# Cross-attention block on one core: the loads and the order of the first 30 microseconds rearranged

## The chip, the cores and the metric

The kernel runs on one core of one Trainium2 chip. The time is device microseconds of one execution; before the change it was 1048.52 us, the median of 3 runs (1047.92 to 1049.07). The engines are named as the profile names them: PE (TensorE, matrix products; PEld is its weight load), DVE (VectorE), ACT (ScalarE), POOL (GpSimd) and SP (SyncE, which issues nearly all DMAs; SPq is that issuing). Each engine runs its own instructions in the order in which the kernel wrote them, and waits at the head of its queue for what the instruction needs.

## The reference: what is computed

All data are float32: x is (16, 1024, 512), the context (16, 64, 512), the condition (16, 512). There are 16 heads of 32.

```python
def _ada_ln(x, c, W_ss, b_ss):
    h = (x - mean(x)) / sqrt(var(x) + 1e-5)
    ss = silu(c) @ W_ss + b_ss
    scale, bias = split(ss, 2)
    return (1 + scale)[:, None, :] * h + bias[:, None, :]

xq  = _ada_ln(x,   t_vec, Wss_q,  bss_q)
xkv = _ada_ln(ctx, t_vec, Wss_kv, bss_kv)
q = xq @ Wq + bq
k, v = split(xkv @ Wkv + bkv)
attn = softmax(q k^T / sqrt(32))          # for each batch and head
out = x + (attn @ v) @ Wp + bp
```

## The kernel before

The 16 x 1024 rows of x are cut into 32 blocks of 512 rows, two to a batch. Block i is held as a tile of 128 partitions by 4 row tiles by 512 features (`x_tiles[i]`). The order of all work is written out by hand: each call adds instructions to the queues of the engines it uses, and they stay in that order. The first blocks have an order of their own (a straight list of calls), then a loop runs over blocks 4 to 29, and a list closes the end. The change lies in the loads at the top and in the straight list, up to the query work of block 0.

What is done there, call by call:

- `load_x(i)`, `load_context(b)`, `load_scale_shift` and the loads beside them issue DMAs on SP. The order before is: condition, x_0 (1 MB in one DMA), four short rows of biases (`brow`), the scale's and then the shift's half of the query side's scale-shift weights (`wss_q`, 1 MB each), `w_q_sb` (1 MB), the first context (256 KB), x_1, both halves of the context side's weights (`wss_kv`), `w_kv_sb` (2 MB).
- `pc` (line 208) transposes the condition on PE; ACT and DVE make silu of it.
- `biases()` transposes `brow` on PE into `pb`; DVE copies it to `bias_t`.
- `q_stats(i)` takes mean and variance of the rows on DVE, two instructions for each row tile. `q_scale(i)` makes 1/sqrt of them: two small instructions on ACT and then four on DVE (lines 279 to 294). `hidden(i, ts)` normalises row tiles on ACT (line 324). `kv_stats`, `kv_scale` and `context_hidden` do the same for the context.
- `scale_shift_rows(name, h)` computes the scale (h = 0) or the shift (h = 1) for all 16 batches as 16 products on PE (`pss`), which the profile lists as 32 instructions, and a copy on DVE; `scale_shift(name, off, h)` transposes that copy on PE (`pst`) and adds the bias on DVE.
- `first_features(ts)` transposes normalised row tiles of block 0 on PE (`pxt`, four transposes for each row tile) and copies them out, even row tiles on ACT and odd ones on DVE.
- `query_weights(0)` multiplies w_q's rows by batch 0's scale: two instructions on ACT and two on DVE.
- `queries(i, o)` makes one 128-feature slice of the queries: 4 products on PE that read all four row tiles (8 instructions in the profile, `pq`). `queried(i, o)` copies the slice to `qt` on ACT and adds the bias; with `later=True` `queries` leaves that call to the list.
- The bias of batch-scaled queries is `bqs`: `query_bias_rows` multiplies the shift by w_q on PE (`pbq`) and copies it on DVE; `query_bias` transposes the copy on PE (`pbt`) and adds b_q on DVE.
- `turn(i)` and `move(i)` transpose the row tiles of later blocks with DVE and DMAs.

PSUM decides some of the order. The pool `ps_m` has four single banks, which `bank(name)` hands out in turn; a bank is written again only when what was read from it has been read:

```python
ring = [0, 1, 2, 3]
def bank(name, k=None):
    if k is None:
        k = ring.pop(0)
        ring.append(k)
    return ps_m.tile([P, TB], F32, tag=f"mm{k}", name=name)
```

The pool `ps_s` has two double banks, used later for the scores; `spare(name)` takes the first half of one.

Of the kernel before, what the change touches and what calls it, by code (L numbers as in the profile page):

```python
# [9 lines left out]
F32 = mybir.dt.float32  # L10
# [5 lines left out]
P = 128  # L16
# [4 lines left out]
def cross_attention_block(  # L21
# [51 lines left out]
    nc = tc.nc  # L73

    B, LQ, H = x.shape
# [3 lines left out]
    NC = H // P  # L79
    HPC = P // DH  # L80
    TB = 512
    NT = TB // P
# [8 lines left out]
    xpool = ctx.enter_context(tc.tile_pool(name="xpool", bufs=2))  # L91
    hpool = ctx.enter_context(tc.tile_pool(name="hpool", bufs=1))
    qpool = ctx.enter_context(tc.tile_pool(name="qpool", bufs=2))
    big = ctx.enter_context(tc.tile_pool(name="big", bufs=1))
# [16 lines left out]
# [5 lines that stand above are left out]
# [15 lines left out]
    def load_context(b):  # L131
        t = kvpool.tile([P, H], F32, tag="ctx", name=f"ctx_{b}")
        nc.sync.dma_start(t, context[b : b + 2].rearrange("b k h -> (b k) h"))
        ctx_tiles[b] = t

    def rows_of(a, i):
        b, s = divmod(i, BPB)
        return a[b, s * TB : (s + 1) * TB, :].rearrange("(t p) h -> p t h", p=P)

    def load_x(i):  # L140

        t = xpool.tile([P, NT, H], F32, tag="r" if i == 3 else "x", name=f"x_{i}")
        nc.sync.dma_start(t, rows_of(x, i))
        x_tiles[i] = t

    def load_residual(i):

# [4 lines left out]

    w_ss = {}

    def load_scale_shift(name, w):
        for j in range(2):
            t = big.tile([P, NC, H], F32, tag=f"big{len(w_ss)}", name=f"wss_{name}_{j}")
            nc.sync.dma_start(t, w[:, j * H : (j + 1) * H].rearrange("(c p) o -> p c o", p=P))
            w_ss[name, j] = t

    load_x(0)

# [3 lines left out]
    for src, n in ((b_ss_q, 2 * NC), (b_ss_kv, 2 * NC), (b_q, NC), (b_kv[0:H], NC)):  # L166
        nc.sync.dma_start(brow[at : at + n, :], src.rearrange("(r f) -> r f", f=P))
        at += n
    load_scale_shift("q", w_ss_q)
    w_q_sb = const.tile([P, NC, H], F32, name="w_q_sb")  # L170
    nc.sync.dma_start(w_q_sb, w_q.rearrange("(c p) o -> p c o", p=P))
    load_context(0)
    load_x(1)
    load_scale_shift("kv", w_ss_kv)
    w_kv_sb = const.tile([P, NC, 2 * H], F32, name="w_kv_sb")
    nc.sync.dma_start(w_kv_sb, w_kv.rearrange("(c p) o -> p c o", p=P))

    b_v_sb = const.tile([P, P], F32, name="b_v_sb")

# [27 lines left out]
    for c in range(NC):  # L207
        nc.tensor.transpose(
            pc[:, c * B : (c + 1) * B], c_sb[:, c * P : (c + 1) * P], ident[:B, :B]
        )  # L210
    pcv = pc[:, : NC * B].rearrange("p (c b) -> p c b", c=NC)
    den = early_tile(P, NC * B).rearrange("p (c b) -> p c b", c=NC)
    nc.scalar.activation(den, pcv, AF.Exp, scale=-1.0)
# [8 lines left out]
    def biases():  # L222
        pb = bank("pb")
        nc.tensor.transpose(pb[:, :NBR], brow, ident[:NBR, :NBR])
        nc.vector.tensor_copy(bias_t, pb[:, :NBR])
# [3 lines left out]
    def scale_shift_rows(name, h):  # L229

        pss = bank(f"pss_{name}_{h}")
        for c in range(NC):
            for p in range(NC):
                nc.tensor.matmul(
                    pss[32 * p : 32 * p + 32, :P],
                    lhsT=silu_t[:, c, :],
                    rhs=w_ss[name, h][:, c, p * P : (p + 1) * P],
                    start=(c == 0),
                    stop=(c == NC - 1),
                )  # L240
        ssr[name, h] = early_tile(P, P)
        nc.vector.tensor_copy(ssr[name, h], pss[:, :P])

    def scale_shift(name, off, h):
        pst = bank(f"pst_{name}_{h}")
        nc.tensor.transpose(pst[:, :P], ssr.pop((name, h)), ident)
        if h == 0:
            ss[name] = const.tile([P, 2 * NC, BW], F32, name=f"ss_{name}")
        at = h * NC
        t = ss[name][:, at : at + NC, :]  # L250
        nc.vector.tensor_tensor(
            t,
            pst[:, :P].rearrange("f (p b) -> f p b", p=NC),
            bias_t[:, off + at : off + at + NC].unsqueeze(2).to_broadcast([P, NC, BW]),
            ALU.add,
        )
        if h == 0:
            nc.vector.tensor_scalar_add(t, t, 1.0)
# [40 lines left out]
    def q_stats(i, ts=range(NT), kvb=None):  # L299

        if ts[0] == 0:
            q_mv[i] = small.tile([P, NT + 1, 2], F32, tag="mvq", name=f"mvq_{i}")
        for t in ts:
            row_stats(q_mv[i][:, t, :], x_tiles[i][:, t, :])
        if kvb is not None:
            row_stats(q_mv[i][:, NT, :], ctx_tiles[kvb])

    def q_scale(i, kvb=None):
        n = NT if kvb is None else NT + 1
        q_rstd[i] = rstd_of(q_mv.pop(i)[:, :n, :], n, "q", i > 2)  # L310
        if kvb is not None:
            kv_rstd[kvb] = (q_rstd[i], NT)
# [15 lines left out]
    def hidden(i, ts):  # L328

        for t in ts:  # L330
            normalise(x_tiles[i][:, t, :], x_tiles[i][:, t, :], q_rstd[i], t)
# [8 lines left out]
    def context_hidden(b):  # L340
        hk = kvpool.tile([P, H], F32, tag="hk", name=f"hk_{b}")
        normalise(hk, ctx_tiles.pop(b), *kv_rstd.pop(b))
        hk_tiles[b] = hk

    def spare(name):
        return ps_s.tile([P, 2, TB], F32, tag="s", name=name)[:, 0, :]
# [111 lines left out]
    bqs_rows = early_tile(P, P)  # L458

    def query_bias_rows():  # L460
        pbq = bank("pbq")
        for c in range(NC):
            for o in range(NC):
                nc.tensor.matmul(
                    pbq[32 * o : 32 * o + 32, :P],
                    lhsT=ss["q"][:, NC + c, :],
                    rhs=w_q_sb[:, c, o * P : (o + 1) * P],
                    start=(c == 0),
                    stop=(c == NC - 1),
                )  # L470
        nc.vector.tensor_copy(bqs_rows, pbq[:, :P])

    def query_bias():
        pbt = bank("pbt")
        nc.tensor.transpose(pbt[:, :P], bqs_rows, ident)
        nc.vector.tensor_tensor(
            bqs,
            pbt[:, :P].rearrange("p (o b) -> p o b", o=NC),
            bq_t.unsqueeze(2).to_broadcast([P, NC, BW]),
            ALU.add,  # L480
        )

    def query_weights(b):
        t = qpool.tile([P, NC, H], F32, tag="wq", name=f"wq_{b}")
        if b:
            scale = ss["q"][:, :NC, b : b + 1].to_broadcast([P, NC, H])
            nc.gpsimd.tensor_tensor(t, w_q_sb, scale, ALU.mult)
        else:
            for c in range(NC):
                scale = ss["q"][:, c, b : b + 1]  # L490
                if c % 2:
                    nc.vector.tensor_scalar_mul(t[:, c, :], w_q_sb[:, c, :], scale)
                else:
                    nc.scalar.mul(t[:, c, :], w_q_sb[:, c, :], scale)
        wq_tiles[b] = t
# [26 lines left out]
    def first_features(ts):  # L522
        if 0 in ts:
            xt_tiles[0] = qpool.tile([P, 4, NC, P], F32, tag="xt", name="xt_0")
        for t in ts:
            pt = bank(f"pxt_{t}")
            for c in range(NC):
                nc.tensor.transpose(
                    pt[:, c * P : (c + 1) * P], x_tiles[0][:, t, c * P : (c + 1) * P], ident
                )  # L530
            dst = xt_tiles[0][:, t].rearrange("p c n -> p (c n)")
            if t % 2:
                nc.vector.tensor_copy(dst, pt)
            else:
                nc.scalar.copy(dst, pt)
        if ts[-1] == NT - 1:
            x_tiles.pop(0)
# [3 lines left out]
    def queries(i, o, later=False):  # L541
        xt, b = xt_tiles[i], i // BPB
        w = wq_tiles.get(b, w_q_sb)
        pq = bank(f"pq_{i}_{o}")
        for c in range(NC):
            nc.tensor.matmul(  # L546
                pq.rearrange("p (g n) -> p g n", g=4),
                lhsT=w[:, c, o * P : (o + 1) * P],
                rhs=xt[:, :, c, :],
                start=(c == 0),  # L550
                stop=(c == NC - 1),
            )
        pq_tiles[i, o] = pq
        if not later:
            queried(i, o)
# [414 lines left out]


    q_stats(0)
    q_scale(0)
    hidden(0, range(NT))
    biases()
    scale_shift_rows("q", 0)
    first_features((0, 1))
    scale_shift("q", 0, 0)
    scale_shift_rows("q", 1)
    first_features((2,))  # L980
    scale_shift("q", 0, 1)
    first_features((3,))
    query_weights(0)
    query_bias_rows()
    load_x(2)
    load_value_bias()
    kv_stats(0)
    kv_scale(0)
    queries(0, 0, later=True)
    context_hidden(0)  # L990
    query_bias()
    queried(0, 0)
    q_stats(1)
    q_scale(1)
    hidden(1, (0, 1))
    queries(0, 1)
    hidden(1, (2, 3))
    for h in range(2):
        scale_shift_rows("kv", h)
    turn(1, range(NT))  # L1000
# [388 lines left out]
```

## Time and profile before

| | |
|---|---|
| median of 3 runs | 1048.52 us |
| profiled execution, its own time | 1047.6 us |
| its span, first to last instruction | 1045.5 us |
| PE busy | 1024.9 us, 98% of the span |
| DVE busy | 863.4 us, 83% |
| ACT busy | 611.0 us, 58% |
| POOL busy | 762.1 us, 73% |
| DMA | 147.50 MB, mean 141 GB/s over the span |
| first long run of PE begins | 10.41 us after the span's start |

All durations come from the profiled execution. Matrix products are pipelined and their ends are modelled, so PE's share is an upper view of its work. A line of a timeline reads: start in us, duration in us, engine, line of the kernel, operation, what is written, what is read, shapes, count; in brackets the idle time before it and what ended that. Where a wait is for several things, the profile names the one that came last by its own records, which can be one that the instruction doesn't depend on.

### The profile page before, as it was taken

To read this page: it belongs to the slowest core of one execution; us is meant where nothing else is said; L and a number is where in the kernel's file an instruction comes from. 1 tells how busy PE (TensorE), PEld (TensorE's weight loads), DVE (VectorE), ACT (ScalarE), POOL (GpSimd) and SP (SyncE) were. 2 spreads that over 40 slices of the span, in tenths; PEclk is the share of its full clock that TensorE was granted. 3 is DMA by queue.
4 is the path that set the end of the run, shared out by engine and by line. 5 is a ranking of instruction groups with operands and counts; after the bars stand their busy time and mean duration, and the time that the engine had idled before them with its cause. 6 is when DMAs were issued, how large, how long until landed. Compare 5 with 4: busy or idle time off the path is not lost.

```text
span 1045.5 us, 22774 instructions
## 1 busy us (share of the span) xinstructions
PE 1024.9 (98%) x8986; PEld 744.5 (71%) x8986; DVE 863.4 (83%) x1150; ACT 611.0 (58%) x940; POOL 762.1 (73%) x495
## 2 busy tenths in 40 slices
PE   6999899999999999999999999999999999999998
PEld 4535577778777778778777787777877777877433
DVE  5798978987798887897889877988778897777993
ACT  3656756665566745665746655666556664565330
POOL 0579786886978866988668897688796886798340
PEclk9999999999999999999999999999999999999999
DMA  9850555343455433545435445354445433335202
GB/s 342 248 185 31 165 165 175 121 146 125 142 172 164 126 99 128 164 155 162 123 87 164 155 142 164 100 158 125 139 148 172 144 121 107 102 112 161 82 31 91
DMA packets 101562, 147.50 MB, mean 141 GB/s; under 512 B 32040, under 2 KB 32192, under 8 KB 101456
## 3 DMA queue, kind: packets, MB, share of 16 engines
q1 hardware_dynamic: 100432, 143.95, 43.1%
q0 software_dynamic: 1024, 2.10, 0.9%
q8 instruction: 71, 1.16, 0.5%
q14 instruction: 35, 0.29, 0.1%
HBM read 78.95 MB, written 34.54 MB: 109 GB/s over the span
## 4 chain that ended last, share of the span: by engine, by line
PE 88%; DVE 4%; POOL 4%; issue 2%; ACT 1%; SPq 1%; DMA 1%; DVEq 0%; POOLq 0%
PE pp L949 32%; PE pq L633 30%; PE po L841 6%; PE ps L681 6%; PE pq L546 5%; PE pp L868 3%; PE pv L434 2%; PE pk L398 2%; POOL s L737 1%; DVE m L693 1%; SPq L516 1%; POOL sum L780 1%; DVE s L737 1%; DVE mb L724 1%; DMA x<-in_x_dram 0%
## 5 line engine op out<-in xcount | busy, mean ns | idle before, releaser
L737 POOL TENSOR_TENSOR s<-s,mb 128x2048 f32<-128x2048 f32 x58 | 263.1, 4563 | 160.1 <-DVE mb L724 156.1
L702 ACT COPY s<-ps 128x1024 f32<-128x1024 f32 x128 | 129.5, 1013 | 111.0 <-DVE m L693 71.7
L693 DVE TRANSPOSE_TENSOR_REDUCE m<-ps 128x32 f32<-128x1024 f32 x128 | 150.8, 1215 | 29.6 <-PE ps L681 29.0
L949 PE MATMUL pp<-w_p_sb,ot 128*128 128x256 f32 x696 | 159.8, 379 | 0.0
L663 ACT ACTIVATE qt<-pq,bias_t 128x256 f32<-128x256 f32 x216 | 89.2, 463 | 111.2 <-PE pq L633 108.7
L963 DVE TENSOR_TENSOR r<-pp,r 128x512 f32<-128x512 f32 x203 | 131.6, 670 | 25.0 <-PE pp L949 17.0
L743 ACT ACTIVATE s<-s 128x2048 f32<-128x2048 f32 x64 | 122.3, 1911 | 43.9 <-POOL s L737 32.5
L949 PEld LDWEIGHTS pp<-w_p_sb,ot 128*128 128x128 f32 x696 | 132.1, 190 | 19.0 <-issue 1.0
L780 POOL TENSOR_TENSOR sum<-s,s 128x2048 f32<-128x2048 f32 x29 | 131.7, 4540 | 3.5 <-ACT s L743 3.4
L949 PEld LDWEIGHTS pp<-WT,s 128*128 128x128 f32 x464 | 83.7, 189 | 54.9 <-issue 32.3
L949 PE MATMUL pp<-WT,s 128*128 128x256 f32 x464 | 115.2, 391 | 0.0
L949 PE MATMUL pp<-WT,ot 128*128 128x256 f32 x464 | 109.8, 379 | 2.4 <-ACT pp L912 2.4
L633 PE MATMUL pq<-xt_sums,wq_sums 128*128 128x256 f32 x432 | 104.9, 386 | 0.0
L633 PE MATMUL pq<-xt,wq_sums 128*128 128x256 f32 x432 | 102.8, 381 | 0.8 <-DVE qt L670 0.8
L633 PEld LDWEIGHTS pq<-xt_sums,wq_sums 128*128 128x128 f32 x432 | 79.8, 190 | 32.4 <-issue 22.6
L633 PE MATMUL pq<-xt,w_q_sb 128*128 128x256 f32 x432 | 102.3, 379 | 0.4 <-ACT pq L645 0.4
L949 PEld LDWEIGHTS pp<-WT,ot 128*128 128x128 f32 x464 | 88.0, 190 | 16.0 <-POOL s L928 3.3
L324 ACT ACTIVATE x<-x,rstdq 128x512 f32<-128x512 f32 x128 | 96.5, 807 | 1.9 <-DVE rstdq L294 1.9
L263 DVE BATCH_NORM_STATS2 bs<-x 128x6 f32<-128x512 f32 x128 | 86.9, 679 | 8.0 <-DMA x<-in_x_dram 8.0
L670 DVE TENSOR_TENSOR qt<-pq,qt 128x256 f32<-128x256 f32 x108 | 40.5, 417 | 63.3 <-PE pq L633 62.8
L633 PEld LDWEIGHTS pq<-xt,w_q_sb 128*128 128x128 f32 x432 | 81.9, 190 | 12.7 <-issue 0.8
L633 PEld LDWEIGHTS pq<-xt,wq_sums 128*128 128x128 f32 x432 | 80.5, 190 | 12.4 <-issue 1.2
(135 smaller groups left out, 1661.0 us busy)
## 6 DMA issues: line engine op xcount, KB each, us to landing
x<-in_x_dram SPq DMA_DIRECT2D x32, 1024.0 KB, 5.7
r<-in_x_dram SPq DMA_DIRECT2D x32, 1024.0 KB, 5.4
xt<-ht SPq DMA_DIRECT2D x464, 64.0 KB, 2.0
out_dram<-r SPq DMA_DIRECT2D x58, 512.0 KB, 3.7
out_dram<-r SPq DMA_DIRECT2D x12, 256.0 KB, 2.0
wss_q<-in_L_xcond_Wss_q_dram SPq DMA_DIRECT2D x2, 1024.0 KB, 8.3
ctx<-in_ctx_dram SPq DMA_DIRECT2D x8, 256.0 KB, 3.1
wss_kv<-in_L_xcond_Wss_kv_dram SPq DMA_DIRECT2D x2, 1024.0 KB
```

The costliest lines, as they stand in the source:

```text
L263: nc.vector.bn_stats(bs, r)
L324: nc.scalar.activation(dst, src, AF.Identity, bias=rstd[:, 1, j : j + 1], scale=rstd[:, 0, j : j + 1])
L633: nc.tensor.matmul(qa[k][:, m * HT : (m + 1) * HT].rearrange("p (g n) -> p g n", g=2), lhsT=a[:, c, m * P : (m + 1) * P], rhs=x[:, :, c, : ...
L663: nc.scalar.activation(dst, src, AF.Identity, bias=bq_t[:, o : o + 1])
L681: nc.tensor.matmul(pss[r // 2][32 * c : 32 * c + 32, r % 2, :], lhsT=kt[rows, c, z * HK : (z + 1) * HK], rhs=qt[rows, c, :], start=True, s ...
L693: nc.vector.tensor_reduce(m_tiles[i][:, z, 2 * e : 2 * e + 2, :], pss[e].rearrange("p r (j a) -> p r j a", a=32), AX.X, ALU.max, apply_tra ...
L702: nc.scalar.copy(s_sb[:, 2 * e : 2 * e + 2, :], pss[e])
L737: eng.tensor_tensor(s_tiles[i, z], s_tiles[i, z], mb_tiles[i], ALU.subtract)
L743: nc.scalar.activation(p, p, AF.Exp, scale=SCALE)
L780: nc.gpsimd.tensor_tensor(t, s_tiles[i, 0], s_tiles[i, 1], ALU.add)
L949: nc.tensor.matmul(acc[k][:, t * HO : (t + 1) * HO], lhsT=rows[:, c, t * P : (t + 1) * P], rhs=cols[:, c, :], start=n == 2 and t == 0 and ...
L963: nc.vector.tensor_add(r, acc[k].rearrange("p (t h) -> p t h", t=2), r)
```

## The change

x_0 is loaded in four DMAs of one row tile each. The scale's weights come first, then w_q, then the shift's weights; w_kv comes in two halves by columns. After the condition's transposes PE runs 20 transposes of the identity into an unused double bank of `ps_s` (`warm(20)`), and 8 more after `biases()`, which moves ahead of `q_scale(0)`. The normalising of block 0 is split in two; the features of all four row tiles and the first slice of the queries come ahead of the shift's products; the second slice comes ahead of `query_bias_rows`; `q_stats(1)` and `q_scale(1)` stand between `query_bias_rows` and `query_bias`; the two `queried` follow, and then the normalising of block 1. `pbq` and `pbt` lie in `spare` instead of a bank of the ring.

```diff
     def load_x(i):
-        t = xpool.tile([P, NT, H], F32, tag="r" if i == 3 else "x", name=f"x_{i}")
-        nc.sync.dma_start(t, rows_of(x, i))
-        x_tiles[i] = t
+        x_tile = xpool.tile([P, NT, H], F32, tag="r" if i == 3 else "x", name=f"x_{i}")
+        for ts in [slice(t, t + 1) for t in range(NT)] if i == 0 else [slice(0, NT)]:
+            nc.sync.dma_start(x_tile[:, ts, :], rows_of(x, i)[:, ts, :])
+        x_tiles[i] = x_tile
...
-    load_scale_shift("q", w_ss_q)
+    load_scale_shift("q", w_ss_q, 0)
     w_q_sb = const.tile([P, NC, H], F32, name="w_q_sb")
     nc.sync.dma_start(w_q_sb, w_q.rearrange("(c p) o -> p c o", p=P))
+    load_scale_shift("q", w_ss_q, 1)
     load_context(0)
     load_x(1)
-    load_scale_shift("kv", w_ss_kv)
+    for j in range(2):
+        load_scale_shift("kv", w_ss_kv, j)
     w_kv_sb = const.tile([P, NC, 2 * H], F32, name="w_kv_sb")
-    nc.sync.dma_start(w_kv_sb, w_kv.rearrange("(c p) o -> p c o", p=P))
+    for j in range(2):
+        half = slice(j * H, (j + 1) * H)
+        nc.sync.dma_start(w_kv_sb[:, :, half], w_kv[:, half].rearrange("(c p) o -> p c o", p=P))
...
+    def warm(n):
+        for _ in range(n):
+            nc.tensor.transpose(idle[:, :P], ident, ident)
+    idle = ps_s.tile([P, 2, TB], F32, tag="s", name="idle")[:, 0, :]
+    warm(20)
...
-        pbq = bank("pbq")
+        pbq = spare("pbq")
...
-        pbt = bank("pbt")
+        pbt = spare("pbt")
...
     q_stats(0)
+    biases()
+    warm(8)
     q_scale(0)
-    hidden(0, range(NT))
-    biases()
+    hidden(0, (0, 1))
     scale_shift_rows("q", 0)
-    first_features((0, 1))
+    first_features((0,))
     scale_shift("q", 0, 0)
+    hidden(0, (2, 3))
+    first_features((1,))
+    query_weights(0)
+    first_features((2, 3))
+    queries(0, 0, later=True)
     scale_shift_rows("q", 1)
-    first_features((2,))
     scale_shift("q", 0, 1)
-    first_features((3,))
-    query_weights(0)
-    query_bias_rows()
     load_x(2)
     load_value_bias()
     kv_stats(0)
     kv_scale(0)
-    queries(0, 0, later=True)
     context_hidden(0)
+    queries(0, 1, later=True)
+    query_bias_rows()
+    q_stats(1)
+    q_scale(1)
     query_bias()
     queried(0, 0)
-    q_stats(1)
-    q_scale(1)
-    hidden(1, (0, 1))
-    queries(0, 1)
-    hidden(1, (2, 3))
+    queried(0, 1)
+    hidden(1, range(NT))
     for h in range(2):
         scale_shift_rows("kv", h)
     turn(1, range(NT))
```

## The prediction

> **What bounds the kernel now.** I read four views of the profile in this order: the page, the waits of TensorE (PE), the chain that ended last in order of time, and the timelines of DVE, ACT and SP over the first 45 us, because every edit lies there.
>
> The page first. The span, PE's row, and the chain's shares by engine:
>
> ```profile
> span 1045.5 us, 22774 instructions
> PE 1024.9 (98%) x8986; PEld 744.5 (71%) x8986; DVE 863.4 (83%) x1150; ACT 611.0 (58%) x940; POOL 762.1 (73%) x495
> PE 88%; DVE 4%; POOL 4%; issue 2%; ACT 1%; SPq 1%; DMA 1%; DVEq 0%; POOLq 0%
> ```
>
> PE is busy for 98% of the span, and the chain is PE for 88%. What PE waited for, longest first (total us, times, longest):
>
> ```profile
> PE pb L224 <- DMA early<-in_L_xcond_bkv_dram: 3.8, 1, 3.8
> PE pss_q L234 <- DVE workq L291: 3.1, 1, 3.1
> PE pc L208 <- DMA early<-in_cond_dram: 2.6, 1, 2.6
> PE pp L949 <- ACT pp L912: 2.4, 1, 2.4
> ```
>
> The first three, 9.5 us, are all before 10.41 us. The other waits in that list add up to some 7 us in more than 1000. So from 10.41 us on PE hardly pauses, and a delay of PE in the first 45 us has nowhere to be absorbed: the work of all later blocks moves with it. I therefore measure the change by one number, the start of the first scale-shift product of the context (pss_kv), since from there on both orders give PE the same work. Before, it starts at 24.86, as the chain in order of time shows (start, us, what):
>
> ```profile
> 10.41 1.94 PE pss_q L234 x32
> 12.35 1.90 PE pxt L528 x8
> ...
> 14.46 1.01 PE pss_q L234 x32
> 15.47 0.59 PE pxt L528 x4
> ...
> 17.68 3.63 PE pq L546 x8
> 21.31 0.11 PE pbt L475
> ...
> 24.86 1.89 PE pss_kv L234 x64
> ```
>
> The reader should see two things. PE runs without a hole from 10.41 to 24.86, so reordering alone can win nothing there. And the first 32 pss_q products took 1.94 us, the next 32 of the same form 1.01; eight transposes took 1.90 first, four 0.59 later. PE starts at about half rate for 4 us: 0.93 + 0.72 = 1.65 us is all that starting warm can save.
>
> What ends the wait at 10.41? The list names a DVE instruction on which pss_q doesn't depend. The tile's DMA answers it (two issues; landing min, median, max):
>
> ```profile
> 3.14 0.95 SPq L158 DMA_DIRECT2D wss_q<-in_L_xcond_Wss_q_dram  x2
> DMA to landing us min/median/max: 7.1/8.3/9.4
> ```
>
> 3.14 + 7.1 = 10.24: the scale's weights land just before PE starts. The shift's land at about 13.0, and w_q at 4.13 + 11.6 = 15.7. The DMA engines' share is 0.9 to 1.1 from 3 us to 30 us.
>
> **The change part by part, up to the first queries.** I call A the start of queries(0, 0). *Rows in four parts:* ctx, a 256 KB load of the same shape, took 0.35 us to issue, so four parts cost 4 x 0.39 = 1.6 us on SP instead of 0.45; the four bias rows and the scale's weights behind them are issued 1.1 us later (4.25 instead of 3.14). SP shows one more thing: the tenth DMA (ctx) waited 1.6 us for the second (x_0) to land. With four parts the tenth is the scale's weights, and it would wait for part 0; with x_0's 1 MB landing 5.0 us after its issue, a quarter is there by about 4.2, so this costs nothing or little. Bounds for the landing of wss_q 0: 4.25 + 5.0 (as x_0 had it, alone) = 9.3, and 4.25 + 7.1 = 11.4. The bytes ahead of it are the same and the engines are full from 3 us, so I take 10.4.
>
> [...]
>
> *Statistics of x_0:* a pair of DVE instructions takes 0.79 us; with parts the last pair alone follows the landing at 6.2, so they end at 7.1 instead of 9.51. The bias transpose (biases) now stands ahead of rstd on DVE: it waits on PE for the 20 idle products (4.75 us at the slow 0.24 each, from 3.2) and ends at about 8.5; rstd is ready at 9.3 instead of 10.96. Two hidden tiles at 0.73 are done at 10.8. All of this hides behind the wait for wss_q 0; if that cover went, it would be 10.8 - 10.4 = 0.4 us late. The second set of 8 idle products (2 us at most) ends before 10.4: cost nothing.
>
> *From there to A* ACT decides, not PE, since it runs its instructions in order:
>
> ```profile
> 11.00 2.93 ACT L324 ACTIVATE x<-x,rstdq 128x512 f32<-128x512 f32 x4 [0.82 <-DVE rstdq L294]
> 16.58 1.34 ACT L494 ACTIVATE wq<-w_q_sb,ss_q 128x512 f32<-128x512 f32 x2
> 21.79 0.69 ACT L568 ACTIVATE qt<-pq,bqs 128x512 f32<-128x512 f32 x1 [0.32 <-DVE bqs L476]
> ```
>
> pss_q warm 10.4 to 11.43; transposes of tile 0 to 12.0; their copy on ACT (0.56) to 12.6; hidden of tiles 2 and 3, queued behind that copy, to 14.1; two weight scalings (w_q lands by 13 to 13.6, in the shift's old place) to 15.4; copy of tile 2 to 16.0. queries(0, 0) reads all four tiles, so A = 16.0 instead of 17.68: 1.7 us won. PE now has holes in this stretch (about 13 to 16) where it had none.
>
> **From A to pss_kv, where it is lost.** Before, this took 24.86 - 17.68 = 7.18 us: two queries and a 0.1 transpose. After, PE has more in between: queries 3.63, the shift's pss_q 1.03, a bare wait for its copy on DVE (0.06 + 0.29), the transpose 0.2, queries 3.63, query_bias_rows (pbq) 1.03, and the copy of that on DVE 0.35. That is A + 10.25 = 26.25. And then comes a new wait. bank() hands out four PSUM banks in turn: counted through the new order, pq_0_0 is the ninth and has bank 0, pq_0_1 bank 3, and pss_kv_0, the thirteenth, bank 0 again. It can't be written until queried(0, 0) has read bank 0 on ACT. queried(0, 0) waits for bqs, and bqs stands on DVE *behind* q_stats(1) and q_scale(1), which themselves stand behind the copy of pbq. Their length is in DVE's timeline:
>
> ```profile
> 21.46 0.29 DVE L476 TENSOR_TENSOR bqs<-pbt,bias_t 128x128 f32<-128x128 f32 x1 [0.84 <-PE pbt L475]
> 21.67 0.68 DVE L263 BATCH_NORM_STATS2 bs<-x 128x6 f32<-128x512 f32 x1
> ...
> 25.64 0.17 DVE L291 SCALAR_TENSOR_TENSOR workq<-workq 128x4 f32<-128x4 f32 x1 [0.69 <-ACT workq L280]
> ...
> 26.24 0.17 DVE L294 SCALAR_TENSOR_TENSOR rstdq<-rstdq,mvq 128x4 f32<-128x4 f32 x1
> ```
>
> Before, bqs came first and the 21.67 to 26.41 = 4.74 us of statistics after it cost PE nothing. After: 26.25 + 4.74 + bqs 0.25 + queried 0.70 + 0.06 of hand-overs = 32.0, against 24.86: +7.15 us. PE idles some 5.5 us (only pbt falls in it). Queued behind pss_kv on PE is everything else: queries(0, 2), the keys, the first scores. x_1 lands before 21.67 in the profile, so the statistics wait for no load.
>
> *After such an idle stretch* PE may be slow again as at 10.41 (there after waits of 3.8 and 3.1 us). Bounds: 0, and the 64 pss_kv products at the slow rate, 2 x 1.94 - 1.89 = 2.0. The row of 10.41 is the nearest, so I take 1.8. Moving hidden(1) after both queried costs nothing: four tiles (2.9 us on ACT) run beside the pss_kv products and queries(0, 2). The later order, w_kv in two halves, pbq and pbt in the score banks: nothing that waits; w_kv is used 10 us after pss_kv.
>
> **The sum.** +7.15 + 1.8 = +8.95. The profiled execution took 1047.6 (span 1045.5 and 2.1 around it), so 1056.55; the median of the runs, 1048.52, is 0.92 above that: 1057.5.
>
> [...] In the trace the rate doubled 4 us after 10.41, and half of those 4 us were transposes, so they do not hinder it; whether they alone release it no run here shows. [...]
>
> If PE starts slow, the row says: pss_q +0.93, first transposes +0.36, so A = 17.3 and 1058.8; part of queries(0, 0) at half rate adds at most 1.9 more (1060.7).
>
> **The rivals.**
> *Not slower: no stall at pss_kv.* If bank 0 were free, or bqs ready when PE gets there, pss_kv would start after pbt, A + 10.45 = 26.45: +1.6, with PE still warm, 1050.1; with wss_q 0 at 9.3, 1049.0. For it: 24.86 shows that the old order kept bqs clear of the statistics, and nothing in the trace forbids an early bqs; against it: each engine of the profile runs in the written order, and the count of banks is fixed. It decides if bqs is done by 25.5 instead of 31.3. Within the 2.1 us that are 0.2%, about what a measurement of this kernel can tell from no change. Chance 6%.
> *Faster by the warm start alone:* the saving is bounded by 1.65, 1046.9, still within 0.2%; more needs wss_q 0 a microsecond earlier as well and no stall. Chance of over 0.2%: 2%.
> *Stall, but PE stays warm through it:* +7.15, 1055.7; with wss_q 0 at 9.3, 1054.6. Chance 20%.
> *Stall and a slow start:* 1058.8 to 1060.7, with wss_q 0 at 11.4 up to 1061.7. Chance 27%.
> *The forecast* (stall, slow after it): 45%.
>
> **How the numbers follow.** The predicted time is the forecast's, 1057.5. Leaving out the first two rivals (8%) and the last tail, the range is 1053.0 to 1061.5. Slower by over 0.2% takes the three cases with the stall, 0.92; same 0.06; faster 0.02.
>
> **What would show it.** In the changed profile: a wait of PE or PEld at pss_kv (scale_shift_rows) of 5 to 6 us put down to ACT's queried or DVE, with DVE running the bn_stats of x_1 in it; queries(0, 0) at about 16.0; 32 pss_q at 1.0 us each time if the warming works; pss_kv at 32, taking 3.7 us instead of 1.89 if PE went slow. PE's later waits unchanged. I am wrong if pss_kv starts before 29, or if a later wait of PE shrinks by as much as the start grew.

## The result and the profile after

The changed kernel takes 1061.9 us, the median of 4 runs (1061.15 to 1062.85), against 1048.57 us for the kernel before in the same comparison: ratio 1.0128, 95% interval 1.0112 to 1.0144, slower by 13.3 us. The forecast was 1057.5 and slower; the time is 0.4 us above the upper end of the range. The profiled execution took 1062.27 us, 14.7 more than the one of before. One execution of e1 below, the profiled one, took 1330.4 us at a granted clock of 0.75; it is left out of e1's times, and of its profile only a wait and the start of pss_q are used.

The page of the changed kernel: PE is as busy by share as it was, and the chain leans less on it (82%, 88% before).

```profile
span 1060.0 us, 22837 instructions
PE 1035.3 (98%) x9014; PEld 752.5 (71%) x9014; DVE 863.6 (81%) x1150; ACT 611.1 (58%) x940; POOL 762.8 (72%) x495
PE 82%; DVE 6%; POOL 5%; issue 2%; ACT 2%; DMA 1%; SPq 1%; DVEq 0%; POOLq 0%; ACTq 0%
```

What PE waited for in it (us in total, times, longest). The first line is new: the context's scale-shift product waits 5.2 us for ACT's copy of the first query slice, as forecast. The second replaces the 3.1 us of before. The third was 2.4.

```profile
PE pss_kv L246 <- ACT qt L580: 5.2, 1, 5.2
PE pss_q L246 <- DMA wss_q<-in_L_xcond_Wss_q_dram: 3.5, 1, 3.5
PE pp L961 <- ACT pp L924: 2.7, 1, 2.7
PE pc L213 <- DMA early<-in_cond_dram: 2.6, 1, 2.6
```

The chain that ended last, in order of time (start, us, what):

```profile
4.48 7.92 DMA wss_q<-in_L_xcond_Wss_q_dram
...
12.54 1.94 PE pss_q L246 x32
14.48 1.06 PE pxt L540 x4
...
19.59 3.67 PE pq L558 x8
23.26 1.05 PE pss_q L246 x32
...
25.01 3.44 PE pq L558 x8
28.45 1.05 PE pbq L476 x32
...
34.47 0.21 DVE bqs L488
...
34.71 0.70 ACT qt L580
...
35.45 3.60 PE pss_kv L246 x64
```

PE starts its long run at 12.54 instead of 10.41, the first queries at 19.59 instead of 17.68, and pss_kv at 35.45 instead of 24.86. Between 29.5 and 34.7 the chain is DVE's statistics of x_1, here in DVE's timeline, with the bias of the queries (bqs) last in the row:

```profile
29.53 0.29 DVE L483 COPY early<-pbq 128x128 f32<-128x128 f32 x1 [1.94 <-PE pbq L476]
29.74 0.68 DVE L275 BATCH_NORM_STATS2 bs<-x 128x6 f32<-128x512 f32 x1
...
34.31 0.17 DVE L306 SCALAR_TENSOR_TENSOR rstdq<-rstdq,mvq 128x4 f32<-128x4 f32 x1
34.39 0.28 DVE L488 TENSOR_TENSOR bqs<-pbt,bias_t 128x128 f32<-128x128 f32 x1
```

Now the clock column shows what it did not show before (its first record here is at 8.17 us; ahead of the first record the column reads 1.00, in the kernel before also over the 32 pss_q products at 10.41 that took 1.94 us). Busy times and granted clock by stretches (PE, PEld, DVE, ACT, POOL busy in us, each with its count; then the clock, the DMA share, GB/s):

```profile
8.00:10.00 2.00, 1.07 (x8) 0.83 (x8) 0.78 (x5) 1.14 (x3) 0.00 (x0) 1.00 0.96 351
10.00:12.00 2.00, 0.00 (x0) 0.00 (x0) 0.00 (x0) 0.83 (x2) 0.00 (x0) 0.90 1.00 369
12.00:14.00 2.00, 1.46 (x28) 1.49 (x32) 0.00 (x0) 0.00 (x0) 0.00 (x0) 0.50 1.03 392
34.00:36.00 2.00, 0.55 (x12) 0.52 (x16) 0.60 (x4) 1.29 (x3) 0.00 (x0) 0.50 0.03 8
131.00:132.00 1.00, 1.00 (x4) 0.79 (x4) 1.00 (x2) 0.62 (x2) 0.15 (x1) 0.52 0.58 174
```

PE ran at half its clock in three stretches: from 11.6 to 18.4, from 32.1 to 38.9 and from 131.1 to 134.5 us. The whole difference can be laid out by the starts of the same products in both profiles: pss_q is 2.13 us later; from there to the first queries 0.22 is won; from there to pss_kv 8.68 is lost (15.86 instead of 7.18); pss_kv itself takes 1.71 more. The sum, 12.3, is unchanged at every product from 42 to 114 us of the kernel before. Then 2.0 come in at product(1, 7), and to the end only 0.2 more. These are the eight products there, first in the kernel before, then in the changed one:

```profile
117.94 1.97 PE L949 MATMUL pp<-WT,ot 128*128 128x256 f32 x8 [2.37 <-ACT pp L912]
...
130.55 3.27 PE L961 MATMUL pp<-WT,ot 128*128 128x256 f32 x8 [2.66 <-ACT pp L924]
```

### The profile page after: what moved, and what is told of

The parts are those of the page before. It is cut to its first block, busy times and chain, and to the rows that moved or that the text cites. A ratio compares the mean times of both kernels' runs of the same rounds, so it can differ in the third digit from the quotient of the medians.

```text
span 1060.0 us, 22837 instructions
## 1 busy us (share of the span) xinstructions
PE 1035.3 (98%) x9014; PEld 752.5 (71%) x9014; DVE 863.6 (81%) x1150; ACT 611.1 (58%) x940; POOL 762.8 (72%) x495
## 4 chain that ended last, share of the span: by engine, by line
PE 82%; DVE 6%; POOL 5%; issue 2%; ACT 2%; DMA 1%; SPq 1%; DVEq 0%; POOLq 0%; ACTq 0%
PE pp L961 29%; PE pq L645 28%; PE ps L693 6%; PE po L853 6%; PE pq L558 4%; PE pp L880 3%; PE pv L446 2%; PE pk L410 2%; POOL s L749 2%; DVE m L705 2%; POOL sum L792 1%; DVE mb L736 1%; DVE s L749 1%; SPq L528 1%; DMA wss_q<-in_L_xcond_Wss_q_dram 1%
```

## The experiments

**The order on DVE.** In e1 the statistics of x_1 and their scale stand behind both copies of the queries:

```diff
     query_bias_rows()
-    q_stats(1)
-    q_scale(1)
     query_bias()
     queried(0, 0)
     queried(0, 1)
+    q_stats(1)
+    q_scale(1)
```

> q_stats(1) and q_scale(1) moved behind queried(0, 1), all else as in the changed kernel. Order theory (the wait of PE at pss_kv is bqs standing behind the statistics of x_1 on DVE): the copy of pbq ends at 29.8 as before, bqs at 30.5, queried(0, 0) at 31.2, so pss_kv starts at about 31.3 instead of 35.45; PE idles only 1 us there and keeps its rate, so pss_kv takes 1.9 instead of 3.6; about 1 us comes back because the scale-shift of the context now waits on DVE behind the statistics. 1061.9 - 4.2 - 1.7 + 1 = 1057, and 1055 if the slow stretch at 131 us goes too. Load theory (the split load of x_0 is the cause, and the order after it only follows): less than 1.5 us is won, 1060.5 or more.

Ratio 1.006 to the kernel before (1.0039 to 1.0081), some 7 us less than the changed kernel's 1.0128 makes; three times of 1054.3, 1055.9 and 1057.6. PE's wait at pss_kv is down to 1.1 us:

```profile
PE pss_kv L246 <- ACT qt L580: 1.1, 1, 1.1
```

The order theory holds; the load theory, which allowed 1.5 us, does not.

**The load.** e2 is the changed kernel with x_0 in one DMA.

```diff
-        for ts in [slice(t, t + 1) for t in range(NT)] if i == 0 else [slice(0, NT)]:
+        for ts in [slice(0, NT)]:
```

> x_0 loaded in one DMA again, all else as in the changed kernel. Order theory: the scale's weights are issued 1.4 us earlier and land at about 10.3 instead of 12.4; PE is then idle for 1.3 us only after the idle products, so pss_q takes 1.0 us instead of 1.94 and queries(0, 0) start at about 16.0 instead of 19.6; the wait at pss_kv stays 5.2 us long. 1061.9 - 3.6 = 1058.3 (2 less if the slow stretch at 131 us goes). Load theory: the order costs next to nothing once the loads are on time, under 1052.

1058.98 us, ratio 1.0092 (1.0077 to 1.0107), by the order theory's 1058.3. In PE's timeline the weights are there at 9.25, and pss_q runs at the full rate:

```profile
9.25 1.08 PE L246 MATMUL pss_q<-wss_q,early 128*32 128x128 f32 x32 [0.73 <-DMA wss_q<-in_L_xcond_Wss_q_dram]
12.04 0.66 PE L540 MATMUL pxt<-ident,x 128*128 128x128 f32 x4 [1.71 <-ACT x L336]
...
16.93 5.44 PE L558 MATMUL pq<-xt,wq 128*128 128x512 f32 x8 [0.88 <-DVE xt L545]
...
34.55 3.39 PE L246 MATMUL pss_kv<-wss_kv,early 128*32 128x128 f32 x64 [5.24 <-ACT qt L580]
```

But pss_kv starts only 0.9 us earlier: with holes of 1.7, 0.7 and 0.9 us before the first queries PE is at half its clock from 13.7 to 20.5, and those queries take 5.44 instead of 3.67. The expected A of 16.0 came at 16.9, for the rows come later with one load. The total came out as expected, the way to it only in part.

**Both edits.** e6 has e1's and e2's together:

```diff
-        for ts in [slice(t, t + 1) for t in range(NT)] if i == 0 else [slice(0, NT)]:
+        for ts in [slice(0, NT)]:
...
-    q_stats(1)
-    q_scale(1)
     query_bias()
     queried(0, 0)
     queried(0, 1)
+    q_stats(1)
+    q_scale(1)
```

> The changed kernel with x_0 in one load and with q_stats(1), q_scale(1) behind queried(0, 1). Theory: the two edits act on different stretches and add up: pss_kv starts 4.2 us earlier than with the one load alone (34.55 there, so 30.3), takes 1.9 us instead of 3.4, and about 1 us comes back behind it: 1059.0 - 4.2 - 1.5 + 1 = 1054.3. What is left over the kernel before, some 5 us, is then the work that the change put on PE between the first query slice and pss_kv without cover: bare hand-overs to ACT and DVE and the holes before the first queries. Rival (the split and the statistics are the whole loss): 1049 to 1050.

1054.1 us, ratio 1.0056 (1.0042 to 1.0070), against 1054.3. The lines of PE's timeline show pss_kv without its slow half:

```profile
18.19 3.67 PE L558 MATMUL pq<-xt,wq 128*128 128x512 f32 x8 [0.88 <-DVE xt L545]
...
29.91 1.95 PE L246 MATMUL pss_kv<-wss_kv,early 128*32 128x128 f32 x64 [1.10 <-ACT qt L580]
...
37.39 2.84 PE L558 MATMUL pq<-xt,wq 128*128 128x512 f32 x6 [1.23 <-ACT qt L580]
```

So about 8 of the 13 us are undone by the two edits, and nearly all of that by the first: e1 alone has 1.0060, e6 1.0056, and their intervals overlap. The theory that the two edits add up is not borne out; the expected time was met, but e2's gain of nearly 4 us does not come on top of e1's.

What stays is 5 to 6 us. In PE's timeline, against the kernel before, 0.6 us of it stand before the first queries (the clock is at half up to 17.0 here too), 4.5 between these and pss_kv, and 1.1 at the query slice at 37.4. The middle part is put down to the order of the products by count, and no run undoes it: the shift's products and pbq (2.1 us) used to fill PE ahead of the first queries while ACT made the rows ready; now they stand behind, with bare hand-overs of 0.4, 0.4 and 1.1 us. The last part is the 1 us that was expected to come back, at another place than expected: PE waits for a query slice's copy, which stands on ACT behind the normalising of block 1, and that begins only at 33.8, when the later statistics are done.

**The bank.** In e4 one more turn of the ring gives pss_kv bank 1.

```diff
     queries(0, 1, later=True)
+    ring.append(ring.pop(0))
```

> One turn of the ring of PSUM banks more behind queries(0, 1), so that the first pss_kv gets bank 1 instead of bank 0, all else as in the changed kernel. Bank theory (pss_kv waits because bank 0 still holds the first query slice): both sets of pss_kv run at about 30.2, at once after pbt, and the wait of some 4 us moves to queries(0, 2), whose bank then holds the second slice until queried(0, 1) at about 36. Queries(0, 2) start at 36.1 instead of 39.05, 1061.9 - 2.9 = 1059. If pss_kv waits for something else (the order on DVE itself, a load): it starts at 35.4 as in the changed kernel, 1061.9.

PE's timeline is as the bank theory has it, to a tenth:

```profile
30.30 1.96 PE L246 MATMUL pss_kv<-wss_kv,early 128*32 128x128 f32 x64
36.19 6.15 PE L558 MATMUL pq<-xt,wq 128*128 128x512 f32 x8 [3.94 <-ACT qt L580]
```

pss_kv at 30.30, the wait moved to queries(0, 2) at 36.19. The time is 1060.57 (1057.8 to 1063.4), not 1059. In the profiled execution (1061.6) those queries, and not pss_kv, now follow the idle stretch, and took 6.15 us instead of 3.6. That the released bank is what pss_kv waited for is shown; of the 2.8 us won at the start of queries(0, 2), their slow run ate 2.4.

**The clock behind the stall.** e5 fills the wait with idle transposes.

```diff
     query_bias()
+    idle = spare("idle_2")
+    warm(36)
     queried(0, 0)
```

> 36 idle transposes on PE between pbt and pss_kv (about 5.3 us at the full rate, so the length of the wait), all else as in the changed kernel. Theory that the idle stretch makes PE slow: pss_kv still starts at about 35.45 but takes 1.9 us instead of 3.6, 1060.2 (1058.2 if the slow stretch at 131 us goes too). Theory that transposes do not count as activity, or that pss_kv is slow for another reason: pss_kv takes 3.6 as in the changed kernel, 1061.9 or more.

```profile
26.25 4.09 PE L219 MATMUL idle<-ident 128*128 128x128 f32 x36
31.66 1.95 PE L246 MATMUL pss_kv<-wss_kv,early 128*32 128x128 f32 x64 [1.32 <-ACT qt L580]
...
51.94 1.22 PE L693 MATMUL ps<-qt,kt 32*32 32x512 f32 x6 [1.97 <-issue]
53.09 5.18 PE L558 MATMUL pq<-xt,wq 128*128 128x512 f32 x8
```

pss_kv takes 1.95 us instead of 3.60, so the slow pss_kv came from the idle stretch, and 4.09 us of transposes in it were enough to keep the rate. (The weights were early in this execution, hence 31.66.) This execution took 1058.9 us, though in it PE waits 2 us for "issue" inside the first scores and runs slow behind that (the query slice at 53.09 takes 5.18 us instead of 3.70); why this wait appears with 36 more instructions stays open. The other three took 1062.3 to 1065.4 us, at mean granted clocks of 0.991 to 0.995 where the profiled one had 0.998: PE lost more to its clock in them, at places that no profile shows. So the fill took the slow pss_kv away, but the median, 1063.8, ratio 1.0127 (1.0098 to 1.0157), is no better than the changed kernel's.

**The clock at the start.** e12 has 20 idle transposes in the second set, not 8.

```diff
-    warm(8)
+    warm(20)
```

> The changed kernel with 20 idle transposes instead of 8 in the second set, which end at about 10.8 instead of 9.1. Theory (PE fell back to the slow rate because it had been idle for 3.5 us when the weights came): pss_q takes 1.0 us instead of 1.94 and queries(0, 0) start about 2 us earlier when the weights are late (17.5), and no later than 16.5 when they are early: 1060. Rival (the rate at the start is free of what came before): pss_q stays at 1.94, 1061.9.

```profile
12.14 1.08 PE L246 MATMUL pss_q<-wss_q,early 128*32 128x128 f32 x32 [1.49 <-DMA wss_q<-in_L_xcond_Wss_q_dram]
...
17.60 3.70 PE L558 MATMUL pq<-xt,wq 128*128 128x512 f32 x8 [1.03 <-ACT xt L547]
...
33.49 3.64 PE L246 MATMUL pss_kv<-wss_kv,early 128*32 128x128 f32 x64 [5.24 <-ACT qt L580]
```

With the weights nearly as late as in the changed kernel, pss_q takes 1.08 and the first queries start at 17.60: the theory of the start, within 0.1. Yet 1062.5 us (1060.5 to 1064.8): of the 2.0 us won at pss_kv only 0.8 are left at the first scores, since the slow stretch lasted to 39.4 here, over more work, and the rest went at product(1, 7), where the wait was 3.5 us.

**The late slow stretch.** e11 puts idle transposes ahead of product(1, 7) in the changed kernel, e15 the same in the kernel before.

```diff
     feature_sums(4)
+    idle = bank("idle_3")
+    warm(14)
     product(1, 7)
```

> The changed kernel with 14 idle transposes ahead of product(1, 7), nothing else. Theory (the wait of 2.7 us there makes PE run slow for 3.4 us behind it): no slow stretch at 131 us, the eight products behind the wait take 2.0 us instead of 3.3, 1.7 us won, 1060.2. Rival (the late 2 us have another cause): 1061.9.

1059.26 us, ratio 1.0095 (1.0080 to 1.0110). The eight products behind the wait take 1.96 us, where they took 3.27:

```profile
126.74 1.75 PE L219 MATMUL idle<-ident 128*128 128x128 f32 x14
129.45 1.96 PE L961 MATMUL pp<-WT,ot 128*128 128x256 f32 x8 [0.97 <-ACT pp L924]
```

The lead over the changed kernel grows by 1.7 us at this place: so much of the 2.0 us there was the clock's. The other 0.3, the longer wait, stays. (The rest of its gain stands before it, where the weights were early.)

> The kernel before with only the 14 idle transposes ahead of product(1, 7). Theory that the 2.4 us wait there makes PE slow in some executions of the kernel before: no time above 1049.5 (the kernel before has some at 1050 to 1050.5), the median 0.3 to 0.7 lower, 1047.9. Rival (it happens only in the changed kernel): the same as before, with the same spread.

1048.38 us, ratio 0.9996 (0.9985 to 1.0006), with 4 of 12 times from 1049.7 to 1050.1. The expectation of a narrower spread failed. The granted clock tells more than the times: in the same comparison 10 of 23 executions of the kernel before have 0.998 and a median of 1050.2 us, the other 13 have 0.999 or more and 1048.2; with the wait filled, all 12 have 0.999 or more. So this wait does cost the kernel before 2 us in some executions, by the clock. The late times of e15 stand at full clock, so something else makes executions longer too, and that stays open.

**One part alone, in the kernel before.** The statistics ahead of query_bias:

```diff
-    query_bias()
-    queried(0, 0)
     q_stats(1)
     q_scale(1)
+    query_bias()
+    queried(0, 0)
```

> The kernel before with only q_stats(1) and q_scale(1) moved ahead of query_bias. Theory that the order of DVE costs only because the copy of pbq comes after both query slices: here the statistics start at 20.6, bqs is ready at 25.6, and only the second half of pss_kv, whose bank holds the first query slice, waits for it: 0.6 us, 1049 to 1050. Theory that this swap alone is the loss: 4 to 5 us, 1053.

1049.12 us, ratio 1.0005 (0.9996 to 1.0014); only the second half of pss_kv waits, 0.4 us. The same swap that costs some 7 us in the changed kernel costs next to nothing here; in the changed kernel the bias product stands behind both query slices, and there the swap becomes a stall.

x_0 in four parts, alone (e10; the first edit), and the same with the rows of biases loaded behind the scale's weights (e14; both edits):

```diff
-        nc.sync.dma_start(t, rows_of(x, i))
+        for ts in [slice(k, k + 1) for k in range(NT)] if i == 0 else [slice(0, NT)]:
+            nc.sync.dma_start(t[:, ts, :], rows_of(x, i)[:, ts, :])
         x_tiles[i] = t
...
+    load_scale_shift("q", w_ss_q, (0,))
     for src, n in ((b_ss_q, 2 * NC), (b_ss_kv, 2 * NC), (b_q, NC), (b_kv[0:H], NC)):
         nc.sync.dma_start(brow[at : at + n, :], src.rearrange("(r f) -> r f", f=P))
         at += n
-    load_scale_shift("q", w_ss_q)
+    load_scale_shift("q", w_ss_q, (1,))
```

> The kernel before with only x_0 loaded in four parts. Theory: the scale's weights are issued 1.4 us later and land about 1 us later (9.1 to 11.1 in the profiles with one load, 10.1 to 12.8 in those with four), and since PE starts with them all of it is lost: 1049.5, pss_q at 11 to 12.5. Rival (the earlier statistics of x_0 pay for it): 1048.4 or less.

> The kernel before with x_0 in four parts as in e10, but the four rows of biases are loaded behind the scale's weights, which are so issued at 3.1 as in the kernel before. Theory that the later issue of the weights costs the 2 us of e10: pss_q back at 10.4, 1048.5. Theory that the four parts themselves slow the stream: as e10, 1050.4.

e10: 1050.37 us, ratio 1.0018 (1.0008 to 1.0028), pss_q at 11.06. e14: 1049.48 us, ratio 1.0008 (0.9995 to 1.0021), with the weights issued at 3.07 and pss_q at 10.01. The split costs some 2 us by itself, but not where it was expected. In e10's profile the context's products start only 0.4 us later than in the kernel before; 2.4 of its 3.5 us come in at product(1, 7), where the wait is longer and the clock is at half from 120.3 to 123.7:

```profile
119.67 3.15 PE L950 MATMUL pp<-WT,ot 128*128 128x256 f32 x8 [3.13 <-ACT pp L913]
```

Nor is it the clock alone: the four executions of e10 at 0.999 or more have a median of 1049.8, the twelve of the kernel before 1048.1. Whether the later issue of the weights is the larger part is not settled; the intervals of e10 and e14 overlap.

w_q ahead of the shift's weights, alone:

```diff
...
-    load_scale_shift("q", w_ss_q)
+    load_scale_shift("q", w_ss_q, (0,))
     w_q_sb = const.tile([P, NC, H], F32, name="w_q_sb")
     nc.sync.dma_start(w_q_sb, w_q.rearrange("(c p) o -> p c o", p=P))
+    load_scale_shift("q", w_ss_q, (1,))
```

> The kernel before with only w_q loaded ahead of the shift's weights. Theory: the shift's weights land at about 15.7 instead of 13, PE needs them at 14.5 and w_q only at 16.6, so PE waits 1.2 us longer and nothing is won: 1049.6. Rival (the query weights are what the start waits for): 1048 or less.

1051.54 us, ratio 1.0025 (1.0014 to 1.0035), more than the 1.2 us expected:

```profile
16.73 1.93 PE L235 MATMUL pss_q<-wss_q,early 128*32 128x128 f32 x32 [1.37 <-DMA wss_q<-in_L_xcond_Wss_q_dram]
18.59 1.12 PE L529 MATMUL pxt<-ident,x 128*128 128x128 f32 x4
...
20.71 1.08 PE L465 MATMUL pbq<-w_q_sb,ss_q 128*32 128x128 f32 x32
```

PE waits 1.4 us for the shift's weights, as expected, and its clock is released only at 20.7 instead of 14.4. The profiled execution ends 5.7 us later than the kernel before's: 0.9 from a later first product, 1.4 from the wait, some 1.8 from the slow rate, and 1.8 at product(1, 7), where the clock is at half from 123.1 to 126.5.

**The idle products, alone** (e8), and with the 14 at product(1, 7) as in e15 (e9):

```diff
...
+    idle = ps_s.tile([P, 2, TB], F32, tag="s", name="idle")[:, 0, :]
+    warm(20)
...
     q_stats(0)
+    biases()
+    warm(10)
     q_scale(0)
     hidden(0, range(NT))
-    biases()
```

> The kernel before with idle transposes alone: 20 behind the condition's transposes, biases() ahead of q_scale(0), 10 more behind it. Theory that PE starts slow because it has been idle, and that transposes count: the first 32 pss_q take 1.0 us instead of 1.94, pss_kv starts at 23.2 instead of 24.86, 1.6 us won, about 1047. Rival (the idle products win nothing, since they do not count or the weights come too late): same as before within 0.5 us.

> As e8, and 14 idle transposes (2 us at the full rate) ahead of product(1, 7), where PE waits 2.4 us for ACT in the kernel before and 2.7 in the changed one, and where the changed kernel's PE then ran slow for 3.4 us. Theory that this wait makes PE slow in some executions (when it falls into one step of the clock gate) also in the kernel before: no slow stretch there in any execution, the times spread less, and the median is another 0.5 to 1.7 us lower, about 1046. Rival (the slow stretch is a matter of the changed kernel's later times alone): as e8.

1048.76 us, ratio 1.0004 (0.9995 to 1.0012), and 1048.19, ratio 0.9995 (0.9985 to 1.0004). PE's timeline of e8 shows why a full-rate start wins nothing:

```profile
9.85 1.08 PE L242 MATMUL pss_q<-wss_q,early 128*32 128x128 f32 x32 [0.35 <-DVE bias_t L233]
12.07 1.36 PE L536 MATMUL pxt<-ident,x 128*128 128x128 f32 x8 [1.14 <-ACT x L332]
...
23.99 1.08 PE L242 MATMUL pss_kv<-wss_kv,early 128*32 128x128 f32 x32
25.58 1.08 PE L242 MATMUL pss_kv<-wss_kv,early 128*32 128x128 f32 x32 [0.51 <-DMA wss_kv<-in_L_xcond_Wss_kv_dram]
```

pss_q is done early, but the rows are normalised no sooner, and at 25.6 the second half of the context's weights is not there yet: 0.8 us ahead at 24 us, 0.1 at 30. No version here beats the kernel before by more than the measurement can tell.

## Why the prediction was right or wrong

*What bounds the kernel* held: the lag of 12.3 us at the context's first products is the lag of every product to 114 us.

*From A to pss_kv* held in each step: 16.0 us predicted, 15.86 measured, with the statistics of x_1 in the wait and bank 0 as its reason (e1, e4). The slow pss_kv behind it was taken at 1.8 and measured at 1.71.

*The landing of the scale's weights* is the term that was mis-sized: taken as 10.4 with bounds of 9.3 and 11.4, it was 12.4. The issue was at 4.48, as worked out; from there the landing took 7.9 us. I took both bounds from one profile and the transfers of it. pss_q started between 10.2 and 13.0 in the seven profiles with four parts and the late issue, and between 9.3 and 11.3 in the eight with one load: in the changed kernel 15 of this transfer's 16 engines had posted their end by 10.6, the last at 12.4, and pss_q started at 12.54. In e5, with the same loads, pss_q started at 10.3 and the first queries at 15.8: there the forecast's start came true. What holds one engine back in some executions stays open.

*The slow start* was a rival with 27%, and it is what happened, for a reason that I had priced at nothing: the second set of idle products "ends before 10.4: cost nothing", but with its end at 9.07 and the weights at 12.4 PE was idle for 3.5 us. Landing and slow start together put A at 19.6 instead of 16.0. That this rival's upper end of 1061.7 lies next to the measured 1061.9 is partly luck: it has the landing a microsecond too early and no term for product(1, 7).

*PE's later waits unchanged* was wrong at one place: the wait at product(1, 7) grew from 2.4 to 2.7 us, and the clock halved behind it, 2.0 us in all, 1.7 of them the clock's (e11). The prediction lists that wait in the profile of before and gives it no price.

In the frame of the profiled execution: +8.95 predicted, +14.67 measured; 3.6 of the difference is A and 2.0 product(1, 7); with either alone the time would have stayed within the range. (The terms from A to the copy of pbq add up to 10.22, not 10.25; nothing turns on it.) The rival that ended not slower failed where its condition said: bqs came at 34.7, not by 25.5. That the warm start could save 1.65 us at best was too much still: e8 saved none, since the rows and the context's weights come next.

On the four parts, the forecast has no term for what they cost by themselves, and e10 alone cost 2.1 us. But its profile shows 0.4 of that at the context's products, so what the parts themselves cost stays open.

## What to carry to other kernels

Before a consumer is queued ahead of its bias to fill the matrix engine, follow the bias through every queue that it stands in, and count which bank its consumer blocks. Work that is moved in front of a gap has to be measured against the work that filled the gap before. And where PE is the bound, cost a pause twice: its length, and the work that can run slow behind it (at pss_kv 5.2 us, and then 1.71 more).

## What the runs showed of the hardware

In the changed kernel PE has nothing but transposes ahead of 8.17 us, from where its clock is recorded as full: the 20 idle float32 ones from 3.15 us took 4.53 us (0.23 each), the 8 behind them 1.23 (0.15 each). So transposes alone released the clock here. e12 agrees (20 in the second set, 2.78 us of them, and pss_q, 1.5 us behind them, took 1.08), and so does e5 with pss_kv at 1.95.

A pause of PE of 2.4 us was followed by slow products in one profile and not in another. Behind the wait at product(1, 7) the eight products took 1.97 us in the kernel before (wait 2.37), 2.50 in e7 (2.40), 3.27 in the changed kernel (2.66), 3.15 in e10 (3.13) and 2.86 in e12 (3.55); with the wait filled down to 0.97 they took 1.96 in e11 and 1.97 in e15. In the records of the changed kernel the slow stretches last 3.41 and 6.83 us and begin at 11.58, 32.06 and 131.05: 20.48 and 98.99 us from one another, 6 and 29 times 3.413. Counted in steps of this length (the step of e9's expectation) from the changes of rate that each profile shows, the longest piece of the wait within one step was 2.66 us in the changed kernel, 2.8 in e10, 2.5 in e12 and 2.1 in e7. In the kernel before, the 2.4 us lay across two steps, 1.2 and 1.1. That this decides is my reading of these five profiles. The wait of e7:

```profile
119.11 2.50 PE L949 MATMUL pp<-WT,ot 128*128 128x256 f32 x8 [2.40 <-ACT pp L912]
```

Here e7 is 1.2 us behind the kernel before (119.11 against 117.94), at the end of the span 2.5 (1048.0 against 1045.5), and its mean granted clock is 0.998 where the other's is 1.000. So the same wait can cost nothing behind it, or more than a microsecond.
